# Issuing VectorE's background operations between a step's scan and its product by C, and the norm's operations in interleaved pairs

## The chip, the cores and the metric

The kernel runs on one NeuronCore of a Trainium2 chip. The metric is the device time of one launch in microseconds (us). The kernel is written by hand in a Python layer that emits the instructions of each engine in program order; every engine then runs its own list strictly in that order and waits on semaphores where an operand or a buffer is not ready. The engines are named as the profile names them: PE (TensorE, matmul; PEld is its weight load), DVE (VectorE), ACT (ScalarE), POOL (GpSimd), SP (SyncE, which here issues the DMAs).

## The reference

Eight images of 64x64 tokens and 96 channels pass two layers, each with a residual. The first is a group norm, a projection to 2 x 192 channels, a depthwise 3x3 convolution with SiLU, a selective scan over 4096 tokens in four directions with 16 states per channel, a norm over the 192 channels, a gate and a projection back. The second is a group norm, an upsampling by Fourier, a small MLP with a quadratic activation and a low-pass with downsampling. Nearly all of the time goes into the scan:

```python
def step(h, inp):                      # per token, in 4 directions, 192 channels, 16 states
    ul, dl, Bl, Cl = inp
    dA = jnp.exp(dl[..., None] * A)
    h = dA * h + (dl * ul)[..., None] * Bl[:, :, None, :]
    y = jnp.einsum('bkdn,bkn->bkd', h, Cl)
    return (h, y)
...
mu = y.mean(-1, keepdims=True)         # the norm and the gate that the change touches
var = ((y - mu) ** 2).mean(-1, keepdims=True)
y = (y - mu) * lax.rsqrt(var + 1e-05) * ln_g + ln_b
y = y * jax.nn.silu(z)
return jnp.einsum('bhwd,cd->bhwc', y, out_proj_w)
```

## The kernel before

**The foreground.** The scan is cut into steps. A step is one tile of 128 partitions (8 channels x 16 states) by T = 1024 tokens; an image has 4 directions x 4 chunks x 24 groups of channels = 384 steps, all eight have 3072. A step goes through the engines as follows. SP issues the load `dub` (delta times u, 512 KB, broadcast over the states). POOL multiplies it by B into `bb` (L1077, four buffers). PE forms the exponent in a PSUM tile `pd` by six matmuls (L1084), ACT turns it into the decay by one Exp (L1092). DVE runs the recurrence over the 1024 tokens (L1099, the scan). Then the state is multiplied by C into `hc`: in two steps of three on DVE (L1105), the scan having been written into `pd` itself, and in every third step (`by_pool`, step number 2 modulo 3) on POOL, the scan having been written into a separate tile `h`. `hold` (L1119) copies the last column into `carry` for the next chunk, on DVE in the first two kinds of step and on ACT in the third; a chunk that is the last of its direction has no such copy. PE sums `hc` over the states (L1138) two steps at a time.

I call a step type 0, 1 or 2 by its number modulo 3. Types 0 and 1 have their product by C on DVE, type 2 on POOL.

**The two `pd` buffers.** `pd` has two buffers, so the matmuls of step i+1 wait until step i-1 is done with its tile: for types 0 and 1 that is the end of product and `hold`, for type 2 the end of the scan.

**The background.** All else (projections, convolutions, gates, norms, the MLP of the image before, the loads and stores that go with them) is written as Python generators, queued in an object `side`. A generator yields a dictionary of what its next piece costs per engine (`pe=0.95`, `act=1.3`, `dve=0.75` and so on) or what it needs (`bank=1`: one of three PSUM banks of the background). Once per step the loop calls `side.advance`, which refills a budget for each engine and lets every active generator emit one further piece if the budget covers it (pieces marked `more` may follow at once). A bank that is given back becomes free at the next `advance`. The background of an image is started at a pace set by its share of about 290 of the 384 steps.

The order of emission in a step i is: load of step i+6, POOL's product by C of step i-1 if that was of type 2, POOL's product by B of step i+3, matmuls and Exp of step i+1, scan of step i, product by C of step i (types 0 and 1), `hold`, `advance` (the background), a filler matmul where PE has little, and the sums of two earlier steps.

**DVE's background operations.** There are five sites: the group norm's statistics `bn_stats` (L474, from a PSUM bank filled by transposes), the convolution's last product (L588), the gate's product (L631), and the two operations of the channel norm, scale by the inverse deviation and by `ln_g` (L715) and bias with the gate (L716). The norm works on 96 partitions in two halves f = 0 and 1, and the second operation reads what the first wrote:

```python
for f in range(HF):
    yield dict(dve=1.4, bank=1 - f, holds=True)
    m, to = (n, t) if f else side.bank("ps")
    # L715: to = flat[f] * ln_g * t, then L716: y[f] = (to + ln_b) * z[f]
```

So each half is one piece, the halves fall in two consecutive steps, and the DVE pieces stand behind `hold` of their step. An image has 8 norm blocks (in the scan of the next image), 16 statistics, 12 convolution and 12 gate products.

**The end.** After the last step `side.drain` emits what is left of the last image without a budget: its last norm blocks, statistics and its MLP.

Of the kernel before, what the change touches and what calls it, by code (L numbers as in the profile page):

```python
# [38 lines left out]
class Side:  # L39
# [12 lines left out]
    def __init__(self, pool):  # L52
        self.pool = pool
        self.free, self.given = list(range(BANKS)), []
        self.urgent, self.hurried, self.later = [], [], []
        self.queue, self.active = [], []
        self.stores = []
        self.alone = {}
        self.begun = 0
        self.caps, self.left = None, {}  # L60

        self.spent = 0.0

# [11 lines left out]
    def emit(self, entry, spare):  # L75

        first = True
        while entry[1] is not None:
            need = dict(entry[1])
            banks, more = need.pop("bank", 0), need.pop("more", False)  # L80
            if need.pop("holds", False):
                spare = 0
            if not (first or more) or (banks and len(self.free) - spare < banks):
                return True
            if self.caps:
                if any(c > self.left[e] for e, c in need.items()):
                    return True
                self.spent += need.get("pe", 0.0)
                for e, c in need.items():
                    self.left[e] -= c  # L90
            entry[1] = next(entry[0], None)
            first = False
        return False
# [15 lines left out]
    def advance(self, caps, more=1, spare=1, taken=0.0):  # L109

        self.caps, self.spent = caps, taken
        if caps:
            self.left = {e: min(self.left.get(e, 0.0) + c, most) for e, (c, most) in caps.items()}
            self.left["pe"] -= taken
        self.free += self.given
        self.given = []  # L120
        for active, spare_ in ((self.stores, 0), (self.hurried, 0), (self.active, spare)):
            for entry in list(active):
                if not self.emit(entry, spare_):
                    active.remove(entry)
            for _ in range(2):
                if self.urgent and active is self.hurried:
                    self.start(self.urgent, self.hurried, 0)
        for _ in range(more):
            if not self.queue or not self.start(self.queue, self.active, spare):
                break  # L130

    def drain(self):
        while self.stores or self.urgent or self.hurried or self.queue or self.active:
# [4 lines left out]
def kernel(ctx: ExitStack, tc: tile.TileContext, a: dict, out: bass.AP):  # L138
# [314 lines left out]
    def stats_items(piece, pad, got):  # L453

        v = {"n": 0}

        def part(g):  # L460
            src = yield from piece(g)
            yield dict(bank=1, pe=0.95, act=0.9 if pad else 0)
            if "st" not in v:
                v["st"] = sm.tile([C, 8, 6], F32, tag="st", name="st")
            n, t = side.bank("pt")
            pt = t[:C].rearrange("p (i a h) -> p i a h", i=4, a=2)
            for i in range(4):
                nc.tensor.transpose(pt[:, i].rearrange("p a h -> p (a h)"), src[:, i, :], ident)
            if pad is not None:
                for wh in range(2):  # L470
                    w0 = 1 + 32 * wh + 4 * g
                    nc.scalar.copy(pad()[:, w0 : w0 + 4, 1:65], pt[:, :, wh, :])
            yield dict(dve=0.6)
            nc.vector.bn_stats(v["st"][:, g, :], t[:C])  # L474
            side.give(n)
            v["n"] += 1

        def last():
            yield {}
            while v["n"] < 8:  # L480
                yield {}
            yield dict(dve=0.2)
            mv = sm.tile([C, 2], F32, tag="mv", name="mv")
            nc.vector.bn_aggr(mv, v["st"].rearrange("p g s -> p (g s)"))
            yield dict(bank=1, pe=0.3)
            n, t = side.bank("pg")
            nc.tensor.matmul(t[:C, 0:1], grp, mv[:, 0:1], start=True, stop=True)
            yield dict(act=0.5)

            dv = sm.tile([C, 1], F32, tag="dv", name="dv")  # L490
            nc.scalar.activation(dv, t[:C, 0:1], AF.Square, scale=-1.0, bias=mv[:, 0:1])
            nc.scalar.activation(dv, dv, AF.Identity, bias=mv[:, 1:2])
            yield dict(pe=0.3, act=0.5)
            nc.tensor.matmul(t[:C, 2:3], grp, dv, start=True, stop=True)
            rs = sm.tile([C, 1], F32, tag="rs", name="rs")
            nc.scalar.activation(rs, t[:C, 2:3], AF.Ln, bias=eps[:C])
            nc.scalar.activation(rs, rs, AF.Exp, scale=-0.5)
            yield dict(act=0.5)
            nb = sm.tile([C, 1], F32, tag="nb", name="nb")
            nc.scalar.activation(nb, t[:C, 0:1], AF.Identity, scale=rs)  # L500
            nc.scalar.activation(nb, nb, AF.Identity, scale=-1.0)
            got.update(rs=rs, nb=nb)
            side.give(n)

        return [(4, 1, lambda g=g: part(g)) for g in range(8)], (4, 1, last)
# [10 lines left out]
    def front(b):  # L516
# [56 lines left out]
        def conv(n, g):  # L573
            yield {}
            while "normed" not in v:
                yield {}
            yield dict(bank=1, pe=0.95)
            bank, t = side.bank("pc")
            for tap in range(9):
                project(t, n, g, w_tap[:, tap, :], tap // 3, tap % 3, start=(tap == 0), stop=(tap == 8))  # L580
                if tap < 8:
                    yield dict(pe=0.87, act=1.4 * (tap == 7), more=True)
            e = bp.tile([128, MB], F32, tag="e", name="e", bufs=4)
            sigmoid_1(t, 1 + n, e)
            yield dict(act=1.3)
            sigmoid_2(e)
            yield dict(dve=0.75)
            nc.vector.scalar_tensor_tensor(e, t, conv_b[:, n : n + 1], e, ALU.add, ALU.mult)  # L588
            side.give(bank)
            yield dict(act=0.7)  # L590
            xt = v["xt"][n]
            nc.scalar.copy(
                xt[:, :, 8 * g : 8 * g + 8].rearrange("p h w -> p w h"), e.rearrange("p (i j) -> p i j", i=8)
            )
            for rows, cs, blk in parts_of(n, g):
                filtered.add((b, n, blk))
                nc.sync.dma_start(
                    u_dram[b][1][cs, MB * blk : MB * blk + MB], e[rows]
                )
# [19 lines left out]
        def gate(n, g):  # L619
            yield {}  # L620
            while "normed" not in v:
                yield {}
            yield dict(bank=1, pe=0.95, act=1.4)
            bank, t = side.bank("pz")
            project(t, n, g, w_z, 1, 1, start=True, stop=True)
            e = bp.tile([128, MB], F32, tag="e", name="e", bufs=4)
            sigmoid_1(t, 0, e)
            yield dict(act=1.3)
            sigmoid_2(e)
            yield dict(dve=0.7)  # L630
            nc.vector.tensor_tensor(e, t, e, ALU.mult)  # L631
            for rows, cs, blk in parts_of(n, g):
                nc.sync.dma_start(z_dram[b][cs, MB * blk : MB * blk + MB], e[rows])
            side.give(bank)
# [13 lines left out]
    def tail(b, keep, pairs=True):  # L648
# [19 lines left out]
        def block(g):  # L668
# [40 lines left out]
            nc.scalar.activation(t[:C], t[:C], AF.Ln, bias=eps[:C])  # L709
            nc.scalar.activation(t[:C], t[:C], AF.Exp, scale=-0.5)  # L710

            for f in range(HF):
                yield dict(dve=1.4, bank=1 - f, holds=True)
                m, to = (n, t) if f else side.bank("ps")
                nc.vector.scalar_tensor_tensor(to[:C], flat[f], ln_g[:, f : f + 1], t[:C], ALU.mult, ALU.mult)  # L715
                nc.vector.scalar_tensor_tensor(  # L716
                    y[f].rearrange("p i j -> p (i j)"), to[:C], ln_b[:, f : f + 1], z[:, f].rearrange("p i j -> p (i j)"), ALU.add, ALU.mult
                )
                side.give(m)
                v["sq"] = f == 0  # L720
            v["gates"] -= 1
            v[g] = y
            if pairs and g >= 4:
# [459 lines left out]
    with tc.manual_schedule():  # L1183
# [20 lines left out]
        for i in range(n + 4):  # L1204
# [36 lines left out]
            if i == 4 or i and i % NT == 0:  # L1241
                side.urgent += side.later
                side.later = []
            if t and t["i"] % 8 == 4:
                before(t)
            if i + FETCH < n:
# [6 lines left out]
                decay(tiles[i + 1])  # L1253
            if t:
                scan(t)
                if not t["by_pool"]:
                    product_c(t)
                hold(t)
# [9 lines left out]
            if ends:  # L1268
                sums(tiles[i - 3 : i - 1])
                if tiles[i - 2]["j"] == 3:  # L1270
                    side.stores.append([g := store(tiles[i - 2]), next(g)])
        up, down, end = mlp(images - 1, keep)
        side.queue += up + down + end
        side.drain()
# [89 lines left out]
```

## Time and profile before

| | |
|---|---|
| median of 3 runs | 11084.81 us (11082.56 to 11093.33) |
| profiled execution: its own time | 11068.84 us |
| profiled execution: its span | 11067.1 us |
| first scan starts, scan of step 96 starts, last scan ends | 141.5, 471.4, 10787.2 us |
| granted TensorE clock over the span | 0.966 |
| DMA, mean rate | 217 GB/s |

The span is that of one execution taken by the profiler; all durations come from it. A row of the groups of instructions gives an instruction's line, engine, operation, tiles and shapes, its count, then the busy time in us and the mean of one in ns, then the idle time of the engine just before it and what ended most of it. A row of the timeline gives start and duration in us, and in brackets an idle time with what released the instruction. The windows give, for each stretch, its length, the busy time and the number of instructions of each engine, the granted clock, the share of time in which the DMA engines were busy, and GB/s.

### The profile page before, as it was taken

The page shows a single profiled execution, that of the slowest core. Times are in us where ns is not written, and L with a number is a line of the kernel's source. Part 1 is how long each engine was busy: PE and PEld are TensorE (multiplying, and loading weights), DVE is VectorE, ACT ScalarE, POOL GpSimd, SP SyncE. Part 2 cuts the span into 40 slices and gives each one's busy share as a digit, 9 for nine tenths or more (in the row PEclk, how much of TensorE's full clock was granted, in tenths as well). Part 3 has the DMA queues.
Part 4 walks back from the last instruction along what each step waited for, and adds up shares of the span by engine and source line. Part 5 has one row for each costly group of instructions (what it writes and reads, how often), then busy time and mean ns, then how long its engine had stood idle before and what let it go on. Part 6 is the DMA issues. An engine that isn't in the chain of part 4 may idle for free. (4 is left out here: it accounts for less than half of the span.)

```text
span 11067.1 us, 152315 instructions
## 1 busy us (share of the span) xinstructions
PE 9616.1 (87%) x52480; PEld 3138.4 (28%) x52480; DVE 9970.5 (90%) x7319; ACT 6865.9 (62%) x10138; POOL 10174.2 (92%) x4674
## 2 busy tenths in 40 slices
PE   7788788998889988999789897898978988888888
PEld 2222223322233222332223322243222422233225
DVE  5999989999899998999999999999999999899990
ACT  5666556666566665666657665576756767566543
POOL 4999999999999999999999999999999999999990
PEclk8999999999999999999999999999999999999998
DMA  6888898898988889888998889888898898988881
GB/s 150 226 209 229 218 226 214 218 228 232 227 212 219 225 233 224 214 226 228 233 221 224 223 234 231 217 217 224 232 230 218 217 226 236 228 213 218 224 206 49
DMA packets 1044528, 2402.22 MB, mean 217 GB/s; under 512 B 293820, under 2 KB 314556, under 8 KB 1043752
## 3 DMA queue, kind: packets, MB, share of 16 engines
q1 hardware_dynamic: 1042776, 2391.45, 86.1%
q8 instruction: 413, 6.77, 0.3%
q14 instruction: 363, 2.97, 0.1%
q10 hardware_dynamic: 976, 1.04, 0.0%
HBM read 1929.05 MB, written 328.73 MB: 204 GB/s over the span
## 5 line engine op out<-in xcount | busy, mean ns | idle before, releaser
L1077 POOL TENSOR_TENSOR bb<-dub,br 128x1024 f32<-128x1024 f32 x3072 | 7177.6, 2359 | 405.4 <-DMA dub<-du 325.2
L1092 ACT ACTIVATE pd<-pd,neg_a 128x1024 f32<-128x1024 f32 x3072 | 3338.0, 1087 | 3341.9 <-PE pd L1084 3326.3
L1099 DVE TENSOR_TENSOR_SCAN pd<-pd,carry,bb 128x1024 f32<-128x1024 f32 x1536 | 3605.1, 2347 | 340.7 <-ACT carry L1119 160.6
L1084 PE MATMUL pd<-dp,sel_b 64*128 64x512 bf16 x18432 | 2608.1, 386 | 1118.7 <-DVE carry L1119 799.7
L1105 DVE TENSOR_TENSOR hc<-pd,cr 128x1024 f32<-128x1024 f32 x2048 | 2508.1, 1225 | 186.4 <-PE py L1138 44.6
L1105 POOL TENSOR_TENSOR hc<-h,cr 128x1024 f32<-128x1024 f32 x1024 | 2415.8, 2359 | 92.0 <-DVE h L1099 68.7
L1138 PE MATMUL py<-hc,sel_r 128*32 128x512 f32 x12288 | 1864.7, 628 | 119.8 <-POOL hc L1105 119.0
L1099 DVE TENSOR_TENSOR_SCAN h<-pd,carry,bb 128x1024 f32<-128x1024 f32 x768 | 1796.5, 2339 | 14.2 <-ACT pd L1092 8.5
L1084 PEld LDWEIGHTS <-sel_b 64*128 64x128 bf16 x18432 | 706.0, 95 | 3661.2 <-issue 1510.6
L1099 DVE TENSOR_TENSOR_SCAN pd<-pd,bb 128x1024 f32<-128x1024 f32 x512 | 1173.8, 2293 | 171.6 <-ACT carry L1119 68.6
L565 PE MATMUL pc<-pad,convr 96*128 96x512 f32 (+1 forms) x2304 | 848.1, 611 | 2.1 <-issue 2.1
L1112 PE MATMUL idle<-xp,ident 128*128 128x384 f32 x1432 | 651.8, 538 | 2.4 <-ACT nb L500 1.7
L1138 PEld LDWEIGHTS py<-hc,sel_r 128*32 128x32 f32 x12288 | 269.6, 110 | 1193.3 <-issue 777.5
L1099 DVE TENSOR_TENSOR_SCAN h<-pd,bb 128x1024 f32<-128x1024 f32 x256 | 583.7, 2280 | 20.9 <-ACT pd L1092 20.6
L1037 POOL TENSOR_TENSOR u<-dl,u 128x512 f32<-128x512 f32 x384 | 489.5, 1275 | 111.2 <-ACT dl L1032 111.2
L852 PE MATMUL ph<-xu,w 96*128 96x500 f32 x960 | 497.2, 620 | 15.8 <-ACT mq L853 10.5
L859 PEld LDWEIGHTS p<-w2q,mq 128*100 128x100 f32 x4800 | 463.8, 169 | 157.0 <-issue 127.4
L859 PE MATMUL p<-w2q,mq 128*100 128x96 f32 x4800 | 502.6, 256 | 2.3 <-ACT mq L853 2.3
L1029 PE MATMUL pv<-e,ident 128*128 128x512 f32 x768 | 464.1, 688 | 31.9 <-ACT pv L1027 30.1
L1039 ACT CAST dp<-pv 128x512 bf16<-128x512 f32 x768 | 451.6, 588 | 7.9 <-PE pv L1038 7.8
L985 PE MATMUL px<-u,xp 64*64 64x512 f32 x1536 | 433.1, 631 | 6.1 <-DMA u<-u 6.0
L1014 PE MATMUL pv<-xd,dt_w 64*64 64x512 f32 x1536 | 429.7, 637 | 1.3 <-ACT dp L1039 0.7
(162 smaller groups left out, 8225.3 us busy)
## 6 DMA issues: line engine op xcount, KB each, us to landing
dub<-du SPq DMA_DIRECT2D x3072, 512.0 KB
u<-u SPq DMA_DIRECT2D x256, 384.0 KB
du<-u SPq DMA_DIRECT2D x768, 128.0 KB
y<-yq SPq DMA_DIRECT2D x768, 128.0 KB
br<-xd SPq DMA_DIRECT2D x256, 256.0 KB
cr<-xd SPq DMA_DIRECT2D x256, 256.0 KB
yp<-y SPq DMA_DIRECT2D x384, 128.0 KB
yp<-u SPq DMA_DIRECT2D x192, 128.0 KB
```

The source lines that it names most:

```text
L565: nc.tensor.matmul(t[rows].rearrange("p (i j) -> p i j", i=8), weights[:, cs], v["pad"][:, 8 * blk + kw : 8 * blk + kw + 8, kh : kh + H], ...
L852: nc.tensor.matmul(t[:, :px], w1[:, m, :], xu, start=True, stop=True)
L859: nc.tensor.matmul(t[:SIDE, C * i : C * i + C], sq[:, m, row], w2q[:, m, :], start=(m == 0), stop=(m == 2))
L1029: nc.tensor.matmul(t, ident, e, start=False, stop=True, skip_group_check=True)
L1037: nc.gpsimd.tensor_tensor(v["u"][:, q, :], dl, v["u"][:, q, :], ALU.mult)
L1077: nc.gpsimd.tensor_tensor(t["bb"], t["dub"], t["got"]["br"], ALU.mult)
L1084: nc.tensor.matmul(pd[:, MB * hf : MB * hf + MB], sel_b[rows, 4 * t["s"] + t["j"]].rearrange("p n c -> p (n c)"), t["got"]["dp", t["q"]][r ...
L1092: nc.scalar.activation(pd, pd, AF.Exp, scale=neg_a[:, t["k"], t["g"] : t["g"] + 1])
L1099: nc.vector.tensor_tensor_scan(t["h"][:, ::step], pd[:, ::step], t["bb"][:, ::step], 0.0 if t["first"] else held, ALU.mult, ALU.add)
L1105: (nc.gpsimd if t["by_pool"] else nc.vector).tensor_tensor(t["hc"], t["h"], t["got"]["cr"], ALU.mult)
L1112: nc.tensor.matmul(p, ident, xp[:, 0:2].rearrange("p k q r -> p (k q r)"), start=True, stop=True)
L1138: nc.tensor.matmul(py[r0 : r0 + 32], sel_r[:, t["j"], :], t["hc"][:, MB * hf : MB * hf + MB], start=(t["j"] == 0), stop=(t["j"] == 3 and t ...
```

## The change

Three things are done. A flag `late` marks the pieces of DVE's background operations. While the loop is past its first 96 steps and before its end (`lagging`), `advance` no longer emits a `late` piece; a new function `slot`, called in each step behind the scan and ahead of the product by C, emits those and nothing else. It does not refill the budget. And the norm takes its second bank first, in a piece of its own, then scales both halves in one piece (f = 0, f = 1) and gates both in the next.

```diff
 class Side:
+        self.behind_scan = self.lagging = False
...
     def emit(self, entry, spare):
             need = dict(entry[1])
+            if (need.pop("late", False) and self.lagging) != self.behind_scan and self.caps:
+                return True
...
+    def slot(self):
+        if not self.lagging:
+            return
+        self.behind_scan = True
+        for active in (self.hurried, self.active):
+            for entry in list(active):
+                if not self.emit(entry, 0):
+                    active.remove(entry)
+        self.behind_scan = False
...
-            yield dict(dve=0.6)
+            yield dict(dve=0.6, late=True)
             nc.vector.bn_stats(v["st"][:, g, :], t[:C])
...
-            yield dict(dve=0.75)
+            yield dict(dve=0.75, late=True)
             nc.vector.scalar_tensor_tensor(e, t, conv_b[:, n : n + 1], e, ALU.add, ALU.mult)
...
-            yield dict(dve=0.7)
+            yield dict(dve=0.7, late=True)
             nc.vector.tensor_tensor(e, t, e, ALU.mult)
...
+            yield dict(bank=1, holds=True)
+            other, to = side.bank("ps")
+            two = (to, t)
+            yield dict(dve=1.4, late=True)
             for f in range(HF):
-                yield dict(dve=1.4, bank=1 - f, holds=True)
-                m, to = (n, t) if f else side.bank("ps")
-                nc.vector.scalar_tensor_tensor(to[:C], flat[f], ln_g[:, f : f + 1], t[:C], ALU.mult, ALU.mult)
+                nc.vector.scalar_tensor_tensor(two[f][:C], flat[f], ln_g[:, f : f + 1], t[:C], ALU.mult, ALU.mult)
+            yield dict(dve=1.4, late=True)
+            for f in range(HF):
                 nc.vector.scalar_tensor_tensor(
-                    y[f].rearrange("p i j -> p (i j)"), to[:C], ln_b[:, f : f + 1], z[:, f].rearrange("p i j -> p (i j)"), ALU.add, ALU.mult
+                    y[f].rearrange("p i j -> p (i j)"),
+                    two[f][:C],
+                    ln_b[:, f : f + 1],
...
-                side.give(m)
-                v["sq"] = f == 0
+            side.give(other)
+            side.give(n)
+            v["sq"] = False
...
+            side.lagging = NT * NCH <= i < n
...
             if t:
                 scan(t)
+                side.slot()
                 if not t["by_pool"]:
                     product_c(t)
                 hold(t)
...
+        side.lagging = False
```

More of the change, by code (lines that the diff above doesn't have):

```diff
@@ L710, in block @@
             nc.scalar.activation(t[:C], t[:C], AF.Exp, scale=-0.5)
+            yield dict(bank=1, holds=True)
+            other, to = side.bank("ps")
+            two = (to, t)
+            yield dict(dve=1.4, late=True)
             for f in range(HF):
-                yield dict(dve=1.4, bank=1 - f, holds=True)
-                m, to = (n, t) if f else side.bank("ps")
-                nc.vector.scalar_tensor_tensor(to[:C], flat[f], ln_g[:, f : f + 1], t[:C], ALU.mult, ALU.mult)
+                nc.vector.scalar_tensor_tensor(two[f][:C], flat[f], ln_g[:, f : f + 1], t[:C], ALU.mult, ALU.mult)
+            yield dict(dve=1.4, late=True)
+            for f in range(HF):
                 nc.vector.scalar_tensor_tensor(
-                    y[f].rearrange("p i j -> p (i j)"), to[:C], ln_b[:, f : f + 1], z[:, f].rearrange("p i j -> p (i j)"), ALU.add, ALU.mult
-                )
-                side.give(m)
-                v["sq"] = f == 0
+                    y[f].rearrange("p i j -> p (i j)"),
+                    two[f][:C],
+                    ln_b[:, f : f + 1],
+                    z[:, f].rearrange("p i j -> p (i j)"),
+                    ALU.add,
+                    ALU.mult,
+                )
+            side.give(other)
+            side.give(n)
+            v["sq"] = False
             v["gates"] -= 1
```

## The prediction

> **What bounds the kernel now.** I read the page's busy times first, then windows of 24 steps, then DVE's groups and its timeline.
>
> ```profile
> PE 9616.1 (87%) x52480; PEld 3138.4 (28%) x52480; DVE 9970.5 (90%) x7319; ACT 6865.9 (62%) x10138; POOL 10174.2 (92%) x4674
> ```
>
> No engine is full, and three are close. The average hides stages, so I cut image 4 into its 16 chunks. Five of them (tail, tail, end of tail, convolution, gates):
>
> ```profile
> core 0: us, PE busy (x) PEld busy (x) DVE busy (x) ACT busy (x) POOL busy (x), PEclk, DMA share, GB/s
> ...
> 5531.10:5624.20 93.10, 77.26 (x388) 21.60 (x392) 83.66 (x68) 52.01 (x81) 90.10 (x44) 0.96 1.00 240
> 5624.20:5715.10 90.90, 76.96 (x403) 21.84 (x396) 84.96 (x71) 53.41 (x82) 89.50 (x43) 0.95 0.92 224
> 5715.10:5801.10 86.00, 72.68 (x469) 24.28 (x471) 83.19 (x55) 47.17 (x65) 82.10 (x39) 0.94 0.81 202
> ...
> 6371.10:6452.20 81.10, 80.62 (x396) 21.83 (x388) 77.20 (x44) 55.91 (x75) 80.56 (x38) 1.00 0.91 231
> ...
> 6618.20:6699.70 81.50, 62.31 (x320) 16.48 (x317) 80.27 (x66) 61.59 (x93) 79.05 (x36) 0.98 0.92 263
> ```
>
> The bound changes: POOL in the tail's first two chunks (97% and 98%), DVE in its third (97%) and under the gates (98%), PE under the convolutions (99%). A saving on DVE is kept only where DVE is the one. Next, where DVE loses time:
>
> ```profile
> L1105 DVE TENSOR_TENSOR hc<-pd,cr 128x1024 f32<-128x1024 f32 x2048 | 2508.1, 1225 | 186.4 <-PE py L1138 44.6 <-DMA dub<-du 1.7 <-DVE pd L1099 1.4
> L716 DVE SCALAR_TENSOR_TENSOR ty<-ps,ln_b,tz 96x512 f32<-96x512 f32 x64 | 47.8, 747 | 2.6 <-DVE ps L715 0.2 <-PE po L746 0.2
> L716 DVE SCALAR_TENSOR_TENSOR ty<-pn,ln_b,tz 96x512 f32<-96x512 f32 x64 | 47.8, 747 | 2.3
> ```
>
> The product by C has 186.4 us of idle time before it, of which little has a releaser: some 139 us over 2048 products, 0.07 us each. Both L716 rows show 0.04. These operations read what the one before wrote. The timeline shows the two cases:
>
> ```profile
> 5036.40 2.34 DVE L1099 TENSOR_TENSOR_SCAN h<-pd,carry,bb 128x1024 f32<-128x1024 f32 x1
> 5039.86 2.36 DVE L1099 TENSOR_TENSOR_SCAN pd<-pd,carry,bb 128x1024 f32<-128x1024 f32 x1 [1.12 <-ACT carry L1119]
> 5042.31 1.23 DVE L1105 TENSOR_TENSOR hc<-pd,cr 128x1024 f32<-128x1024 f32 x1
> 5043.45 2.35 DVE L1099 TENSOR_TENSOR_SCAN pd<-pd,carry,bb 128x1024 f32<-128x1024 f32 x1
> 5045.83 1.23 DVE L1105 TENSOR_TENSOR hc<-pd,cr 128x1024 f32<-128x1024 f32 x1
> 5046.97 0.74 DVE L588 SCALAR_TENSOR_TENSOR e<-pc,conv_b,e 128x512 f32<-128x512 f32 x1
> 5047.63 2.34 DVE L1099 TENSOR_TENSOR_SCAN h<-pd,carry,bb 128x1024 f32<-128x1024 f32 x1
> ```
>
> The scan from 5039.86 ends at 42.22 and its product starts at 42.31, a gap of 0.09. The product ends at 43.54, but the next scan has started at 43.45, and L588 and the scan behind it overlap by 0.08 too. So a dependent neighbour costs 0.07 + 0.08 = 0.15 us more than an independent one. The second row shows the larger loss: 1.12 us before a type 0 scan. PE explains it:
>
> ```profile
> 5035.03 2.84 PE L565 MATMUL pc<-pad,convr 96*128 96x512 f32 x6
> 5037.81 0.82 PE L1084 MATMUL pd<-dp,sel_b 64*128 64x512 bf16 x6
> ```
>
> The `pd` buffer was released with the `carry` copy at 5036.48, but PE was in a convolution until 37.87. Counted over the whole timeline behind step 96, DVE loses 447 us before type 0 scans, 82 before type 1, 34 before type 2; in 385 of the 447 PE was still busy when the buffer was released. Release to end of Exp takes 2.01 us at the least, and the type 2 scan that covers it 2.26 from start to start: 0.25 of slack. The stall before a type 0 scan, by where the preceding three steps had background on DVE: nowhere 0.61 us (685 cases), type 0 alone 0.21 (68), type 1 alone 0.12 (73), type 2 alone 0.08 (69), several 0.04 or less (96). Background mostly fills a stall.
>
> **The change, part by part.** Nothing is removed: 559 background operations stand behind step 96 in both programs' orders.
>
> *(a) The gap ahead of the product.* In the changed order, 127 type 0 and 114 type 1 steps carry background between scan and product; 176 type 2 steps have no product on DVE and gain nothing (before: 145, 152, 115). 241 x 0.15 = 36 us of DVE time. Below zero is excluded for the gap itself; 0.19 (0.105 in the timeline's upper quarter plus 0.08) would make 46.
>
> *(b) The norm's pairs.* Two scales, then two gates: no neighbour reads its neighbour's result. 61 blocks x 2 x (0.04 + 0.08) = 15 us of DVE time.
>
> [...]
>
> *(c) What is kept of (a) and (b).* Only where DVE bounds. In the changed order, the tail's third chunk and the two chunks with most gates hold 84 of the 241 steps, and the former 21 of the 61 blocks: 84 x 0.15 + 42 x 0.12 = 18 us. The rest falls where POOL or PE is at 97 to 99%, or where a stall takes it back: 0 of it, at most the other 33.
>
> *(d) Release of `pd`.* Product and `hold` come up to 0.74 us (a norm pair 1.4) later, and PE's matmuls of the step after next wait for them, with PE's background queued behind. I cost this at nothing: in before's "type 0 alone" the background likewise precedes the release of type 1's buffer, and the stall is 0.21 instead of 0.61, since PE works off its backlog meanwhile. If that cover fails, see the slower rival.
>
> *(e) New waits in DVE's queue.* A late input now holds up product, release and next scan. Measured against the end of the scan in the same step, Exp for L588 and L631 ended at most 0.14 us after it (0.1 us in all), the transposes of L474 in 6 of 112 cases (20.8 us in all, but there the product itself stood waiting for PE). The norm's Exp would be late by 9.5 us, but its pair now comes a step later. 0, at most 20. The gate's store on SP is issued a little earlier: 0.
>
> *(f) The background shifts.* The norm's extra bank piece costs a step per block, and the changed order runs some 10 to 18 steps later: POOL's adds of the tail (L687) are 8, 4, 4 per chunk instead of 8, 6, 2, and two gates move into the last chunk (DVE 74.1 of 75.9 in that window). Two adds of 1.5 us leave the 98% window: up to 3 x 7 images = 20 us, at least 0, since the third chunk is nearly full. I take the middle, 10.
>
> *(g) The end.* One norm block more (4 x 0.7 us) is left to the drain, mostly beside a DMA round trip of 4.7 us (store of `y` after 10793.61, add at 10798.26): +1, at most +3.
>
> Sum: -18 - 10 + 1 = -27 us on a span of 11067.1, so 11040. The median of the runs is 17.7 above that span; 11084.8 - 27 = 11058.
>
> **The rivals.**
>
> *Eaten.* The stalls before type 0 scans grow by what DVE saves, as POOL and PE are no faster, and (f) gives nothing. For it: POOL's 97% in many windows. Against: the DVE windows. 11085, give or take 15. That the change doesn't act falls in here, but the order shows it acting.
>
> *Slower: the held release.* Place: the type 0 scan. If background ahead of a product gives PE no time to catch up, only type 2 fills that stall. In the changed order 816 of 992 triples have none at type 2: 816 x 0.61 + 176 x 0.06 = 508 us against 447, +61. Less the 18 kept: +43, 11128. It decides from 18 us of such loss on, a third of its price. For it: PE waits 800 us for that release already:
>
> ```profile
> PE pd L1084 <- DVE carry L1119: 799.7, 750, 6.5
> ```
>
> Against: type 0 alone, in (d).
>
> *Faster throughout.* All of (a), (b) and (f): 51 + 20 - 1 = -70, 11015. Part of the first case's chance, as its far end.
>
> **How the numbers follow.** A measurement of this kernel tells about 0.2% (22 us) from no change: 11063 to 11107. Forecast with its far end 0.45, eaten 0.26, held release 0.29. The forecast lies near the edge of no change, as the rivals' lower ends do; these cancel. Faster 0.45, same 0.26, slower 0.29. The range goes from the far end, 11015, to the held release, 11128. The likeliest case alone has 11015 to 11080.
>
> **What would show it.** Idle time before L1105's successor (line 1128) falls from 186 to about 170 us (241 x 0.07 less), and that before the norm's second operation to nothing. The type 0 stall stays at 0.2 or less where background precedes a product of the triple; 0.5 or more there would prove the held release. In the second tail chunk POOL's busy time falls by 3 us, and the chunk with it; if only the stalls grow, the saving was eaten. The prediction is wrong if PE's wait for `carry` grows by more than 50 us, or if a schedule shift makes the chunks of transposes and convolutions (87 and 81 us) longer.

## The result and the profile after

| | before | after |
|---|---|---|
| median of 10 runs each | 11082.74 us (11079.36 to 11093.33) | 11111.78 us (11095.68 to 11123.79) |
| ratio, 95% interval | | 1.0026 [1.0016, 1.0035] |
| span of the profiled execution | 11067.1 us | 11093.9 us |
| its parts: up to step 96, to the end of the last scan, rest | 471.4, 10315.8, 279.9 | 475.3, 10344.5, 274.0 |

The change makes the kernel slower by 0.26%, some 29 us. The time lies inside the predicted range, on the other side of no change from the forecast. In the profiles the loop behind step 96 is longer by 28.7 us and the end shorter by 5.9. The 3.9 us ahead of step 96, where both programs are the same, show what a single profile can be off by.

Busy times of the engines on the page of after:

```profile
PE 9651.1 (87%) x52512; PEld 3159.7 (28%) x52512; DVE 9939.9 (90%) x7319; ACT 6871.9 (62%) x10138; POOL 10173.5 (92%) x4674
```

DVE runs the same 7319 instructions, and is busy for 30.6 us less (9970.5 before): a moment in which two of them overlap counts once, and they overlap by 390.8 us in all, by 361.9 before. Its groups in after: the scan with carry, the product by C, the two gates.

```profile
L1122 DVE TENSOR_TENSOR_SCAN pd<-pd,carry,bb 128x1024 f32<-128x1024 f32 x1536 | 3607.4, 2349 | 410.7 <-ACT carry L1142 175.8 <-ACT pd L1115 172.8 <-POOL bb L1100 54.2
L1128 DVE TENSOR_TENSOR hc<-pd,cr 128x1024 f32<-128x1024 f32 x2048 | 2505.3, 1223 | 177.3 <-PE py L1161 47.2 <-DMA dub<-du 4.8 <-DVE pd L1122 1.4
...
L733 DVE SCALAR_TENSOR_TENSOR ty<-pn,ln_b,tz 96x512 f32<-96x512 f32 x64 | 47.2, 738 | 0.0
...
L733 DVE SCALAR_TENSOR_TENSOR ty<-ps,ln_b,tz 96x512 f32<-96x512 f32 x64 | 46.3, 723 | 0.0
```

Idle time before the product fell by 9.1 us (by 14.8 without the waits for PE's sums and for `dub`, which grew), that before the gates from 4.9 to nothing. With the busy time that is 44.6 us of DVE time saved, of the 51 that (a) and (b) promised. It was all spent again ahead of the scans. The row of before that answers to the first one:

```profile
L1099 DVE TENSOR_TENSOR_SCAN pd<-pd,carry,bb 128x1024 f32<-128x1024 f32 x1536 | 3605.1, 2347 | 340.7 <-ACT carry L1119 160.6 <-ACT pd L1092 122.1 <-POOL bb L1077 51.0
```

Idle time ahead of this form of scan grew by 70.0 us, and over all four forms by 72.7. 72.7 - 44.6 = 28.1 us, about the loop's loss. The loop's time is DVE's busy and idle time, so this account has to close: it says where the time stands and not why. A second profile of after has 679 us ahead of the scans where this one has 620 and before 547, so its sizes are rough. The part that grew most is the wait for Exp, that is for PE's matmuls (122.1 to 172.8 in these rows).

Where in an image? The five chunks of image 4 that the prediction showed, in after (length, then busy time of each engine, then the granted clock):

```profile
core 0: us, PE busy (x) PEld busy (x) DVE busy (x) ACT busy (x) POOL busy (x), PEclk, DMA share, GB/s
5539.80:5636.50 96.70, 79.67 (x378) 20.36 (x370) 81.68 (x67) 51.70 (x79) 91.57 (x44) 0.92 1.01 233
5636.50:5724.30 87.80, 75.01 (x430) 22.84 (x426) 82.23 (x69) 51.57 (x79) 82.66 (x40) 0.98 0.85 212
5724.30:5818.10 93.80, 74.72 (x402) 23.31 (x398) 84.47 (x58) 49.23 (x68) 87.81 (x42) 0.93 0.86 209
6392.00:6473.60 81.60, 77.10 (x378) 21.07 (x374) 75.58 (x44) 56.27 (x80) 79.05 (x37) 0.98 0.88 220
6636.70:6718.60 81.90, 64.91 (x322) 16.81 (x319) 80.92 (x67) 67.62 (x103) 77.70 (x36) 0.94 0.95 263
```

The chunks start at other times than before's, but at the same steps. In the second, POOL's add has moved out as (f) said, and the chunk is 3.1 us shorter. The third is 7.8 longer, with DVE busy for 90% of it where it had been 97%. Over images 1 to 7 the means say the same: first 95.1 to 97.0, second 91.8 to 88.8, third 86.5 to 92.9; the chunk behind these went from 84.5 to 80.5.

What is new stands among PE's waits. Before (engine, line, what released it: us in all, times, longest):

```profile
PE pm L699 <- DVE ty L716: 4.4, 14, 0.5
...
PE po L740 <- DVE ty L716: 1.5, 2, 0.9
```

After:

```profile
PE pd L1107 <- DVE carry L1142: 737.4, 674, 6.5
...
PE pm L712 <- DVE ty L733: 44.0, 22, 3.2
...
PE idle L1135 <- DVE st L487: 14.1, 7, 2.0
PE po L763 <- DVE ty L733: 12.0, 7, 1.8
```

The wait for `carry` (the held release) fell from 799.7 to 737.4. But PE now waits for background operations of DVE, summed over all such rows: 18.1 us before, 95.7 after (ACT: 2.5 and 16.1). One of them, in after's timeline, DVE first (start, duration):

```profile
5588.54 2.35 DVE L1122 TENSOR_TENSOR_SCAN pd<-pd,carry,bb 128x1024 f32<-128x1024 f32 x1
5590.80 0.72 DVE L733 SCALAR_TENSOR_TENSOR ty<-ps,ln_b,tz 96x512 f32<-96x512 f32 x1
5591.44 0.74 DVE L733 SCALAR_TENSOR_TENSOR ty<-pn,ln_b,tz 96x512 f32<-96x512 f32 x1
5592.10 1.21 DVE L1128 TENSOR_TENSOR hc<-pd,cr 128x1024 f32<-128x1024 f32 x1
```

and PE beside it:

```profile
5588.14 0.39 PE L1061 MATMUL pv<-dp,minus 128*128 128x512 bf16 x1
5591.58 1.10 PE L712 MATMUL pm<-ty,cen_w 96*96 96x512 f32 x2 [3.05 <-DVE ty L733]
5592.51 1.70 PE L714 MATMUL pm<-ty,cen_w 96*96 96x512 f32 x2
5594.14 1.46 PE L1107 MATMUL pd<-dp,sel_b 64*128 64x512 bf16 x6
```

PE is ahead of DVE. The gates in the slot give back their PSUM bank; `advance` of the same step hands it to the next norm block, whose first matmul (L712) so stands in PE's list in that step and waits for a gate that sits behind a whole scan. The `pd` matmuls of the foreground are queued behind it. In before the gates stood behind `hold`, their bank became free an `advance` later, and PE's wait there was 0.5 us at the longest (L699 above). I call pieces that take what the slot released in the same step *close followers*.

### The profile page after: what moved, and what is told of

Read it like the earlier page. It is cut to its first block, busy times and chain, and to the rows that moved or that the text cites. A ratio compares the mean times of both kernels' runs of the same rounds, so it can differ in the third digit from the quotient of the medians.

```text
span 11093.9 us, 152284 instructions
## 1 busy us (share of the span) xinstructions
PE 9651.1 (87%) x52512; PEld 3159.7 (28%) x52512; DVE 9939.9 (90%) x7319; ACT 6871.9 (62%) x10138; POOL 10173.5 (92%) x4674
## 5 line engine op out<-in xcount | busy, mean ns | idle before, releaser
L1107 PE MATMUL pd<-dp,sel_b 64*128 64x512 bf16 x18432 | 2619.0, 388 | 1040.7 <-DVE carry L1142 737.4
L1135 PE MATMUL idle<-xp,ident 128*128 128x384 f32 x1464 | 675.5, 544 | 23.4 <-DVE st L487 14.1
L1008 PE MATMUL px<-u,xp 64*64 64x512 f32 x1536 | 438.2, 634 | 16.1 <-DMA u<-u 16.1
```

The lines of the kernel that those rows point to most:

```text
L1107: nc.tensor.matmul(pd[:, MB * hf : MB * hf + MB], sel_b[rows, 4 * t["s"] + t["j"]].rearrange("p n c -> p (n c)"), t["got"]["dp", t["q"]][r ...
L1135: nc.tensor.matmul(p, ident, xp[:, 0:2].rearrange("p k q r -> p (k q r)"), start=True, stop=True)
```

## The experiments

Each kernel was timed in five rounds against the kernel before on the same chip; ratios are to that. A single profile varies by some 30 us from the next, so sums over a profile are shown only where they differ by a factor. "PE's waits" means PE's idle time ended by background operations of DVE.

The theories were: the place itself costs (held release of `pd`); close followers cost; the norm's pairs cost; it is the chance of one arrangement; or the clock makes a small wait large.

**The place of the slot.** From after, everything else in the same order on every engine, the slot's operations go behind `hold`:

```diff
                 scan(t)
-                side.slot()
                 if not t["by_pool"]:
                     product_c(t)
                 hold(t)
+                side.slot()
```

> The changed kernel with the slot moved behind the product by C and the carry copy: the other engines' orders are those of the changed kernel instruction for instruction, DVE's background alone goes back to its old place in the step. Theory H (the place costs: background ahead of the product holds back the release of pd, and PE and all behind it wait): near before, ratio to before 0.999 to 1.001. Theory S (the shifted schedule costs, the place gains some 18 us as predicted): 1.0026 or up to 0.0016 above it. If each has half: 1.0013.

And from before, all of its order kept, product and `hold` are emitted behind the background of their step (past step 96, types 0 and 1):

```diff
+                behind = i >= NT * NCH and not t["by_pool"]
+                if not behind:
...
+            if t and behind:
+                product_c(t)
+                hold(t)
```

> The kernel before with all background of steps of types 0 and 1 emitted between scan and product by C, from step 96 on: PE, ACT, POOL and SP keep the order of before, only DVE's background goes ahead of the product. H: near the changed kernel, ratio to before 1.002 to 1.003. S: 0.9983 to 1.000, for the gaps ahead of the products are filled and nothing else moves.

Measured: 1.0074 [1.0062, 1.0086] with the slot late, which neither theory had, and 0.9999 [0.9990, 1.0007] for the new place with the old order. DVE's groups in the second:

```profile
L1099 DVE TENSOR_TENSOR_SCAN pd<-pd,carry,bb 128x1024 f32<-128x1024 f32 x1536 | 3608.2, 2349 | 395.6 <-ACT carry L1119 180.9 <-ACT pd L1092 160.6 <-POOL bb L1077 44.9
L1105 DVE TENSOR_TENSOR hc<-pd,cr 128x1024 f32<-128x1024 f32 x2048 | 2503.7, 1223 | 135.2 <-PE py L1138 13.0 <-DVE pd L1099 2.7 <-PE pd L1084 1.4
```

The idle time ahead of the product is 51 us smaller than before's 186.4, but 31.6 of that is a shorter wait for PE's sums (44.6 to 13.0). The other 20, with 17.9 us less of busy time, are what the place saves, 38 us. The stall ahead of the scans with carry is 55 larger. In this order the place does what it says to DVE and is worth nothing. With the slot late PE waits longer for the same followers:

```profile
PE pm L712 <- DVE ty L733: 74.1, 22, 4.6
...
PE idle L1135 <- DVE ty L733: 26.2, 7, 3.7
PE idle L1135 <- DVE st L487: 24.5, 8, 3.3
PE po L763 <- DVE ty L733: 24.0, 7, 3.4
```

All such rows sum to 188.7 us, against 95.7 in after, and the time is 0.4 to 0.5% above after's. This is the cleanest pair for close followers: one order of instructions on all other engines, longer waits, a longer time. DVE's place differs between the two as well.

**Slot and pairs apart.** From after, `side.lagging = False` throughout (pairs without the slot), and the old norm pieces, marked `late` (slot without pairs):

```diff
-            side.lagging = NT * NCH <= i < n
+            side.lagging = False
```

> The norm in interleaved pairs with its extra piece for the bank, but no slot: all background is emitted by advance, behind the carry copy, as before. H: 0.999 to 1.001. S: the norm's extra step per block is what shifts the schedule, so 1.002 to 1.003, unless the slot's own rule shifts it.

```diff
+                yield dict(dve=1.4, bank=1 - f, holds=True, late=True)
+                m, to = (n, t) if f else side.bank("ps")
```

> The slot with the norm of before (each half scaled and gated in one piece, marked late). H: 1.002 to 1.003, as the place is that of the changed kernel. S: nearer to before than the changed kernel if the norm's extra step is the shift, 0.999 to 1.001; near 1.0026 if the slot's own rule is the shift.

Measured: pairs alone 1.0019 [1.0010, 1.0028] with PE's waits at 9.9 us, slot alone 1.0011 [1.0002, 1.0020] with 109.3. The two costs add up to after's, and the pairs cost theirs without a new wait of PE for background. But 0.11% is less than what a shift alone can do (0.16%, below).

**The followers a step later.** From after, what the slot gives back is free one `advance` later; in the second, a generator that emitted in the slot also sits out the `advance` of that step; in the third, the first with the norm's extra bank step taken out:

```diff
-        self.given = []
+        self.given, self.slow = self.slow, []
...
+        kept, self.given = self.given, []
...
+        self.slow, self.given = self.given, kept
```

> The changed kernel, but a PSUM bank that is given back in the slot is free for others one advance later (as it was before the change). Theory F (followers too close: advance hands a bank, freed by the slot in the same step, to a matmul, and PE in its order waits for the DVE operation of that very step): idle time of PE ended by background DVE falls from 96 us (18 before the change) to under 35, ratio to before 1.0005 to 1.0015. Theory S (only the later schedule of the background costs): 1.0026 or more, as banks come later still.

```diff
+                if id(entry) in self.passed:
+                    continue
...
+                if entry[1] is not need:
+                    self.passed.add(id(entry))
```

> As the one with banks a step later, and a generator that emitted in the slot sits out the advance of that step, so that the copy on ACT behind the convolution's product comes a step later as before the change. F: ACT's idle time ended by background DVE falls from 16 us to under 5, ratio to before 1.000 to 1.0012. S: 1.0026 or more.

```diff
-            yield dict(bank=1, holds=True)
+            yield dict(dve=1.4, bank=1, holds=True, late=True)
...
-            yield dict(dve=1.4, late=True)
```

> The changed kernel with the slot's banks a step later (1.0000) and without the norm's extra piece for the bank: slot, pairs and place stay. F and S together: the followers' waits are gone and a part of the shift too, 0.9980 to 0.9998, below before. If the new place itself costs (as the place with pairs at 1.0031 hints): 1.001 to 1.003.

Measured: 1.0000 [0.9991, 1.0009], 1.0040 [1.0027, 1.0052], 1.0028 [1.0019, 1.0037], with PE's waits at 5.8, 10.8 and 7.1 us. The first looked like the proof: waits gone, loss gone. The other two have no such waits either and lose as much as after. So close followers aren't the whole loss, and one arrangement alone proves little here. The third fell where its text had put "the new place itself costs".

**The pairs without the extra step, and with the new place.** From before, the norm's scales in one piece that takes the bank itself, its gates in the next; then the same on top of the new place with the old order:

```diff
+            yield dict(dve=1.4, bank=1, holds=True)
+            other, to = side.bank("ps")
+            two = (to, t)
...
+            yield dict(dve=1.4)
```

> The kernel before with the norm in two pieces as before, but the first scales both halves and the second gates both; no piece for the bank alone, no slot. The pairs alone with the extra piece gave 1.0019. If the extra step per norm block (the shift) was its cost: 0.999 to 1.0007. If the pairs themselves cost (two PSUM banks held through both pieces, both halves done late): 1.0012 to 1.0025.

> The new place on the order of before (0.9999 when alone) together with the pairs without an extra step: both savings of DVE time (36 and 15 us) with neither the shift nor close followers. If they are kept where DVE bounds, as I predicted of them: 0.9975 to 0.9995. If DVE's savings are eaten by stalls: 0.9995 to 1.001.

And before with nothing but an empty piece, `yield {}`, ahead of the norm's loop:

> The kernel before with one empty step in each norm block ahead of its VectorE pieces, and nothing else: no slot, no pairs. Theory S (a later background costs by itself): 1.0008 to 1.002, about the difference of pairs with the extra step (1.0019) and without (1.0007). If lateness is free and only close followers cost (F): 0.9992 to 1.0005.

Measured: 1.0007 [0.9997, 1.0017], 1.0031 [1.0020, 1.0041], 0.9993 [0.9984, 1.0001]. The extra step and the shift of the order behind it cost nothing, though PE's waits are 32 us in that kernel. The new place with pairs lies above both of its texts' ranges.

**The new place, three times.** In the traces, three couples of these kernels run the same instructions in the same order on PE, ACT and POOL (but for a few neighbours on PE), and differ in where DVE's background stands: before and the new place; pairs without the step, with and without the new place; and pairs alone with followers later, which is the same order with the operations in the slot. None has PE's new waits. The stall before a type 0 scan is measured as in the prediction, by what the three steps before it had of background on DVE:

| couple, old place to new | ratio | background at type 0 alone | no background | all type 0 stalls |
|---|---|---|---|---|
| before, new place | 1 to 0.9999 | 0.22 to 0.30 us (68 cases) | 0.61 to 0.63 | 447 to 491 us |
| pairs without the step, new place and pairs | 1.0007 to 1.0031 | 0.24 to 0.48 (31) | 0.62 to 0.62 | 470 to 505 |
| pairs alone, followers a step later | 1.0019 to 1.0040 | 0.50 to 0.90 (99) | 0.70 to 0.71 | 533 to 601 |

The scans with carry of the third couple (pairs alone, then followers later):

```profile
L1122 DVE TENSOR_TENSOR_SCAN pd<-pd,carry,bb 128x1024 f32<-128x1024 f32 x1536 | 3606.5, 2348 | 392.5 <-ACT carry L1142 191.3 <-ACT pd L1115 136.0 <-POOL bb L1100 57.0
L1131 DVE TENSOR_TENSOR_SCAN pd<-pd,carry,bb 128x1024 f32<-128x1024 f32 x1536 | 3607.5, 2349 | 452.5 <-ACT carry L1151 193.8 <-ACT pd L1124 173.6 <-POOL bb L1109 77.3
```

The stall grows where background now holds back a product, and hardly elsewhere; most of the growth is again the wait for Exp. That is the held release. With the norm's halves in turn it took no more than the place saved. With the norm in pairs the place cost 0.24% and 0.21%, 23 to 27 us; the intervals of the second couple lie apart, those of the third all but do. Why it is dearer there, by the pairs themselves or by the order that they bring, no run separates.

**The chance of one arrangement.** After once more, and both kernels with another pace of the background (`total * at / 290` becomes 280 or 300), which moves background pieces to other steps:

> The changed kernel itself once more, as a measure for the others beside the same runs of before: 1.0016 to 1.0035 by its first measurement (1.0026) under every theory.

> The kernel before with the background of an image started by a pace of 280 instead of 290 steps, so a little earlier, and nothing else. If it is lateness that costs (S): 0.998 to 1.0005. If any shift of the background costs because the order of before happens to meet the foreground well: 1.0008 to 1.003. This gives the size of what a neutral shift does, against which all the other ratios are to be read.

> The changed kernel with a pace of 280 instead of 290. Before with 280 gave 0.9984. F: the followers stay too close in this arrangement too, so 1.001 to 1.003, above before with 280 by 0.002 to 0.004. If the changed kernel's loss was chance of one arrangement: 0.998 to 1.000.

> The changed kernel with a pace of 300. F: 1.002 to 1.004, above before with 300 by 0.002 to 0.004. Chance of one arrangement: the same as before with 300.

> The kernel before with a pace of 300, a neutral shift the other way: 0.9985 to 1.0015 if such shifts are worth some 0.0015 either way, above 1.001 if a later background costs.

| pace | before | after |
|---|---|---|
| 280 | 0.9984 [0.9975, 0.9993] | 1.0047 [1.0035, 1.0060] |
| 290 | 1 | 1.0026 and 1.0035 [1.0023, 1.0047] |
| 300 | 1.0000 [0.9991, 1.0009] | 1.0044 [1.0031, 1.0057] |

The loss is there at every pace, so it isn't the chance of one. Before with 280 is the fastest kernel of the study and owes nothing to the change.

**The slot ahead of the scan.** From after, `side.slot()` before `scan(t)`, so that the followers wait for no scan:

> The changed kernel with the slot moved ahead of the scan: the other engines' orders are those of the changed kernel instruction for instruction, as they were with the slot behind the carry copy (1.0074; PE idle 189 us for background DVE) and in the changed kernel (1.0026 and 1.0035; 95 us). Third dose on one order. F: PE's idle time ended by background DVE falls below 40 us and the ratio to before to 0.999 to 1.0015, less what DVE now waits for late inputs (up to 0.001). If the wait is not the cause but the arrangement: 1.0026 to 1.0035 again.

Measured: 1.0191 [1.0177, 1.0205]. PE's waits are down to 8.2 us, but DVE now stands before operations whose input is late, with the scan queued behind:

```profile
DVE e L601 <- ACT e L527: 157.5, 86, 18.2
...
DVE e L644 <- ACT e L527: 80.9, 55, 3.0
```

After has 42.7 and 0.2 there. What I had allowed for this was far too small, and the run can't decide on followers as a whole. The tail's three chunks and the one behind them, which have little of that wait, take 356.7 us an image here, 359.2 and 358.1 in after's two profiles and 361.1 with the slot late, where PE's waits are 8, 95 and 189 us. But before has 357.8 there, so of these only the late slot stands out.

**The clock.** From step 96 to the end of the last scan the granted clock stood at one half for 601 us in before, and for 724 and 771 us in after's two profiles. Both kernels with more filler matmuls (issued at `side.spent < 1.6` instead of `< 1.0`), to see whether this time changes and the loss with it:

> The changed kernel with the filler matmul issued in every step in which the background's PE work is under 1.6 us instead of 1.0 (900 fillers instead of 732). [...] If this half clock is what turns PE's added waits into lost time: half-clock time falls by 50 us or more and the ratio by 0.001 or more, to 1.000 to 1.0025. If the clock is a mere companion of the stalls: 1.003 or more, as PE has more to do.

> The kernel before with the same fillers (848 instead of 716). Half clock as the amplifier: 0.997 to 0.9995, half-clock time below 560 us. A companion only: 1.000 to 1.002.

Measured: after 1.0030 [1.0020, 1.0041], before 0.9995 [0.9986, 1.0004]. Time at half clock, over the same part of the run, was 676 us in after and 567 in before (granted clock over the span 0.963, against 0.961 and 0.958 in after's two profiles, and 0.967 against 0.966). The loss stayed what it was, but so did most of the difference between the two kernels, so the fillers alone don't decide. Two other kernels do better: banks a step later spends 775 us at half clock and the empty step 727 (granted clock 0.959 and 0.961), as much as after, at ratios of 1.0000 and 0.9993. Half clock by itself isn't the loss.

**All runs together.** By what a kernel has:

| place of DVE's background | norm | close followers | kernels | ratios | mean |
|---|---|---|---|---|---|
| old | in turn | no | before, empty step, paces 280 and 300, filler | 0.9984 to 1.0000 | 0.9994 |
| new | in turn | no | new place | 0.9999 | |
| old | pairs | no | pairs without the step, pairs alone | 1.0007, 1.0019 | 1.0013 |
| new | pairs | no | banks later, banks later without the step, new place with pairs, followers later | 1.0000 to 1.0040 | 1.0025 |
| new | in turn | yes | slot alone | 1.0011 | |
| new | pairs | yes | after twice, its paces 280 and 300, its filler | 1.0026 to 1.0047 | 1.0036 |
| old | pairs | longer | slot behind `hold` | 1.0074 | |

All kernels with pairs but one lie above all without pairs and followers. The group of after overlaps with the one that has pairs and the new place without followers. So that the change costs is shown, that the new place costs with pairs is shown by two couples, and that long waits for followers cost is shown by the late slot. How much of after's 29 us falls to each isn't. Banks a step later, at 1.0000 with pairs and the new place, isn't explained; no run has its order with the old place. The slot ahead of the scan is left out, as DVE's late inputs set its time.

## Why the prediction was wrong

Three terms of the sum failed: (c), which kept 18 us where about 1 was left; (d), which put the held release at nothing; and (e), which put new waits at nothing and looked for them on DVE alone. The forecast had the sign wrong because its gains were spent and its costs were left out.

**(a) and (b), the DVE time: right.** 44.6 us of the 51, or 50 without the longer waits for PE's sums and for `dub` ahead of the product. Some 20 us of it is idle time; the rest shows as busy time, as operations now overlap.

**(c), "18 us" kept: wrong.** With the old order the new place kept nothing: 0.9999 [0.9990, 1.0007] is 1 us, at most 11. The rival "eaten" describes it. I had argued from windows in which DVE was at 97%, but a full engine in a window of 24 steps still has a partner that is nearly full, and its stall before the next scan took the time back.

**(d), the held release put at nothing: wrong.** I argued that PE works off its backlog meanwhile. In the three couples of one order, the stall before the type 0 scan grew by 0.09, 0.24 and 0.40 us where background at type 0 alone precedes the product. The first was paid for by what the place saved; with the norm in pairs it wasn't, and the place cost 23 to 27 us. The rival "held release" had the mechanism, if not the size: it had asked for 61 us of stall, and after has some 32 more than before's 447. The test that I named, a stall of 0.5 us or more, was bad, as the order changes the stall too: at type 0 alone it is 0.67 us in after (51 cases), but also 0.72 with the slot behind `hold` (51) and 0.50 with pairs alone at the old place (99). Only kernels of one order can be compared.

**(e), "0, at most 20": wrong.** I looked only at what DVE would wait for. I did not ask who waits for the operations moved, in which step they hand back a bank, and that PE, ahead of DVE and in order, would meet that bank's next user with its `pd` matmuls behind. That is 78 us more idle on PE and 14 on ACT. The late slot, with 93 more again on PE, costs 0.39% to 0.48% over after's two measurements, so a wait of that kind isn't free. What it costs in after isn't known: the means of after's group and of the group with pairs and the new place differ by 0.11%, 12 us, less than the spread inside the latter.

**(b) again: the pairs.** I priced them as a gain or nothing. At the old place, without any of PE's new waits, the two kernels with pairs lie at 1.0007 [0.9997, 1.0017] and 1.0019 [1.0010, 1.0028]. Why stays open. The extra step isn't it (0.9993 alone). Two banks held longer would be an answer, but kernels that hold banks an `advance` longer still (1.0000, 1.0040, 1.0028) are no slower than the new place with pairs (1.0031). Two DVE operations back to back in one step, or the order that the pairs bring, would be others; no run separated those.

**(f), "-10": half right.** The second tail chunk gained its 3 us per image. The third gave back 6.4, and the chunk behind it gained 4.0.

**(g):** +1 predicted, -5.9 measured.

**The signs of error named** were a wait for `carry` 50 us larger (it fell by 62) and longer chunks of transposes and convolutions. That list lacked the row that did grow.

## What to carry to other kernels

When an operation is moved on its engine, look first at what it releases and what it now stands in front of: a planner that hands a buffer on in the same step puts the next user into the list of an engine that is ahead, and everything of that engine stands behind: here PE, whose idle time for DVE's background went from 18.1 to 95.7 us. In a pipeline whose busiest engines are at 87, 90 and 92% (PE, DVE and POOL), as here, gaps closed on one of them may be worth nothing until the next wait is shown to shrink too; move the operations with all other orders kept, and time that, before building on the saving. Do so in more than one order: the same move was free in one and cost 0.2% in two others. And where a neutral change of pace is worth 0.16%, and kernels with the same parts differ by 0.4%, one arrangement proves nothing: vary something neutral and compare groups.

## What the runs showed of the hardware

The granted clock was 0.966 over the span of before and 0.961 over that of after. From step 96 to the end of the last scan it stood at one half in 133 stretches of before, 601 us in all, and in 164 of after, 724 us. The six `pd` matmuls of a step show what that is worth to them: in after they took 0.82 us in the median of the 2907 steps in which they ran wholly at a granted clock of 1, and 1.46 us in the 54 in which they ran wholly at one half. The timeline above has one of the latter: at 5594.14, behind PE's 3.05 us of waiting, they took 1.46 us, with a granted clock of 0.50 in that stretch; at 5587.38, ahead of the waiting, 0.82 us with 1.00. With more filler matmuls the time at half clock was shorter (676 us against 724 and 771 in after, 567 against 601 in before). What brings the clock down was not shown. More time at half clock did not mean a longer run: banks a step later had 775 us of it at a ratio of 1.0000, before 601 and after 724.
